# Two changes in one: an attention-and-experts kernel gets a new start, a new split of its shared half steps and a new final layernorm

## The chip, the core and the metric

The kernel runs on one core of one Trainium2 chip, in float32 throughout. The metric is the device time of one execution in microseconds, as the median of several runs. The engines are TensorE (PE in the profile, its weight loads PEld), VectorE (DVE), ScalarE (ACT), GpSimd (POOL) and SyncE (SP), which here only issues DMAs.

## The reference

The input is 16 sequences of 512 tokens of 128 numbers. Cut to what matters:

```python
# attention
q, k, v = silu(x @ Wq), silu(x @ Wk), x @ Wv            # 16 heads of 8
q, k = [concat(t * cos(theta * pos), t * sin(theta * pos)) for t in (q, k)]
out = ((q @ k.T) * causal_mask) @ v                     # per head, no softmax
out = (out @ Wo) * sigmoid(x @ G1 @ G2)
x = layernorm(x + layernorm(out) * gamma + beta)        # eps 1e-5
# mixture of experts
xn = x * rsqrt(mean(x * x) + eps)
probs = softmax(xn @ router_w.T)
top2, weights = top_k(probs, 2)                         # weights normed to sum 1
routed = for each of 8 experts, its first 1280 tokens:  (silu(xg @ rg) * (xg @ ru)) @ rd, times weight
shared = (silu(x @ sg) * (x @ su)) @ sd                 # hidden width 1024
x = layernorm(x + shared + routed)
```

## The kernel before

The tokens are cut into NT = 64 tiles of P = 128, NC = 4 to a sequence, B = 16 sequences of N = 512. Nearly all of the program's order is written by hand: inside a `manual_schedule` each engine takes its instructions in the order in which the Python code emits them.

**Constants (from L214).** SP and ACT issue the first loads. theta's row is spread over the partitions by a matmul `pth` (L280); `angles(c, th)` (L299) makes, for the tile position c, the angle theta·pos reduced to ±π with nine VectorE operations, and `sines(c)` takes cosine and sine on ScalarE into `cst_tok`. ScalarE folds G1·G2 into the projection weights `W` (L288). Four padded buffers `vpad` are zeroed, two on POOL (L274) and two on ScalarE (L277). `beginning(t)` puts the sines of tiles 1, 2, 3 ahead of `project` in the first iterations.

**Attention loop, t = -2 .. 64.** An iteration handles several tiles at different depths: `project(t + 2)` (the matmul `pq`, L418, then on ScalarE Silu into `qk`, Tanh for the gate, copies into `vpad`; on VectorE the rotation into `hat`), `turn_over(t + 1)` (transposes `pt`, L458, and ScalarE's copies kT, q2, qT), `energies(t)` (`pe`, then VectorE's causal mask into `et`), `values(t - 1)` and `remember(t + 1)` (matmuls `pst`, L479, which go into the running state through VectorE and a POOL addition, L490). Every fourth iteration starts a generator `after(b)` for a finished sequence: Wo, gate, first layernorm, residual, second layernorm, transposition into x1T, router logits. It is advanced some steps per iteration. In it, POOL takes reciprocal roots as a power of -0.5 (`rstd_of`, L113) and one more such power for the router's root mean square (`rms`, L594). `route(b0, b1)` is another generator, for the sequences 0-5, 6-11 and 12-15: softmax, top 2, ranks by matmuls `pin` (L690) that wait for VectorE's `both` (L679), slot numbers. When it has ended, `scatter_behind` issues on POOL, two an iteration, indirect DMAs that write the tokens' rows into `xg_dram` by slot.

**Shared expert.** Its work is cut into 384 half steps in the list `feed`: for each sequence eight pairs of `gate_half` (matmul pg, L137, then ScalarE's Silu `sl`, L139) and `up_half` (matmul pu, L150, then VectorE's product `h`, L151), and eight `down_half` (four matmuls into pd, L160; two make a tile, which VectorE adds into x1T, L165). The downs of a sequence stand behind the first two pairs of the next. `shared(t)`, twice an iteration, takes a half step if the sequence at the head of `feed` is ready:

```python
ready[b] = t + (6 if b else 10)
```

After the loop a while loop goes on with one half step per pass until the last sequences are normed, routed and scattered. There a pass count `waited` decides when a routing generator that has said "wait" goes on to its matmuls.

**Experts.** `load_expert(0)` fetches weights and the scattered rows `xg`; `clear_rows` (VectorE) blanks the unused rows in three parts, `turn_rows` (L904, L905) transposes them into xgT. Then 8 experts of three parts each; rows go back through an indirect DMA into `y_dram`.

**Finish.** The half steps that are left are done one per pass. From ten half steps after the last return of rows, every second pass adds one of 32 sums (`add_up`, L961, two per sequence) and every pass takes one or two steps of the final layernorm (`an_end`), in lots of tiles: `finish_lot` (one step per tile of statistics, one for the reciprocal root, then nb, L985, and one step per tile of ScalarE's output `res`, L988, the last with the output's DMA). When the last gate has been issued, ScalarE's Sqrt takes the place of POOL's power (`rstd_by_root`, L119, L121).

```python
                an_end()
                if begun % 2 == 1 or not feed:
                    an_end()
```

PSUM has three banks for g, three for u and two for d (pd, ept, ped) in the experts and the finish.

Of the kernel before, what the change touches and what calls it, by code (L numbers as in the profile page):

```python
# [19 lines left out]
P = 128  # L20
# [27 lines left out]
def tile_kernel(  # L48
# [44 lines left out]
    rms = keep.tile([P, NT], F32, name="rms")  # L93
# [101 lines left out]
    with ExitStack() as ph:  # L195
# [21 lines left out]
        with tc.manual_schedule(engines=ORDERED):  # L217
            th_row = cst.tile([1, D + HALF], F32, name="th_row")
            nc.sync.dma_start(th_row, theta.unsqueeze(0))
# [15 lines left out]
            nc.vector.memset(half_pi, math.pi / 2)  # L235
            warm = cst.tile([P, 1], F32, name="warm")
# [36 lines left out]
            for vp in vpads[:2]:  # L273
                nc.gpsimd.memset(vp, 0.0)  # L274

# [3 lines left out]
            pth = ps_w.tile([P, D + HALF], F32, tag="w", name="pth")  # L279
            nc.tensor.matmul(pth, ones[0:1, :], th_row, start=True, stop=True)  # L280
            th_sb = wk1.tile([P, D + HALF], F32, tag="w", name="th_sb")
            nc.scalar.copy(th_sb, pth)
# [3 lines left out]
            for vp in vpads[2:]:  # L286
                nought(vp.rearrange("p a b d -> p (a b d)"), 640)
# [3 lines left out]

            cst_tok = cst.tile([P, NC, 2, 16, 2, 8], F32, name="cst_tok")
            scratch = hp.tile([P, 10, D + HALF], F32, tag="h", name="scratch")
            turns_of = wk1.tile([P, D + HALF], F32, tag="o", name="turns_of")
            nc.vector.tensor_scalar(turns_of, pth, 1.0 / (2.0 * math.pi), None, ALU.mult)

        def angles(c, th):  # L299

            a, size, k, whole = scratch[:, c], scratch[:, NC + c], scratch[:, 8], scratch[:, 9]
            both = ((slice(0, D), pos[:, 0, c : c + 1]), (slice(D, D + HALF), pos[:, 1, c : c + 1]))
            for m, at in both:
                nc.vector.tensor_scalar(k[:, m], turns_of[:, m], at, MAGIC, ALU.mult, ALU.add)
            nc.vector.tensor_scalar(whole, k, MAGIC, -C1, ALU.subtract, ALU.mult)
            for m, at in both:
                nc.vector.scalar_tensor_tensor(a[:, m], th[:, m], at, whole[:, m], ALU.mult, ALU.add)
            nc.vector.tensor_scalar(k, k, MAGIC, -C2, ALU.subtract, ALU.mult)
            nc.vector.tensor_tensor(a, a, k, ALU.add)
            nc.vector.scalar_tensor_tensor(size, a, -1.0, a, ALU.mult, ALU.max)  # L310
            nc.vector.tensor_scalar(a, a, -PI_BELOW, PI_BELOW, ALU.max, ALU.min)
# [4 lines left out]
        def sines(c):  # L316

            for s, (from_, scale, bias) in enumerate([(scratch[:, NC + c], -1.0, half_pi), (scratch[:, c], 1.0, 0.0)]):
# [13 lines left out]

        with tc.manual_schedule(engines=ORDERED):
            angles(0, pth)
            sines(0)
            angles(1, th_sb)
            same(0)

# [3 lines left out]
            nc.gpsimd.tensor_tensor(causal[:, 0:1], scratch[:, 0, 0:1], zcol, ALU.mult)  # L342
# [13 lines left out]
            for at in (0, HALF):  # L356
                rows = causal[at : at + HALF, :]
                nc.gpsimd.affine_select(
                    rows, rows, pattern=[[1, HALF]], compare_op=ALU.is_ge, fill=0.0, base=0, channel_multiplier=-1
                )  # L360
            expi = cst.tile([P, E], I32, name="expi")
# [27 lines left out]
        def beginning(t):  # L389

            if t == -1:
                sines(1)
            elif t == 0:
                angles(2, th_sb)
                sines(2)
            elif t == 1:
                angles(3, th_sb)
                sines(3)

# [15 lines left out]

# [697 lines left out]
```

## Time and profile before

| | |
|---|---|
| median of 17 runs | 854.47 us (852.81 to 857.84) |
| the profiled execution | 853.75 us |
| its span | 852.0 us |
| TensorE busy | 815.5 us, 96% of the span |
| VectorE busy | 538.0 us, 63% |
| ScalarE busy | 414.2 us, 49% |
| POOL busy | 361.2 us, 42% |
| mean granted TensorE clock | 0.991 |

The span runs from the first to the last instruction. Each engine's busy time is the sum over its instructions; a busy TensorE hides the others wherever they keep up with it. The page also cuts the span into 40 slices of 21.3 us with the busy tenths of each engine and the clock granted to TensorE. A line of the waits names who waits, in which line, for whom: the total, how many times, and the longest.

### The profile page before, as it was taken

Reading aid. Unit: us, or ns where it says so; the run is one execution under the profiler, and the core shown is the slowest. Engines: PE = TensorE matmul, PEld = TensorE weight load, DVE = VectorE, ACT = ScalarE, POOL = GpSimd, SP = SyncE. Lnnn points to the kernel's source line nnn. Section 1 sums busy time; section 2 is a strip of 40 time slices with the busy share of each in tenths; the row PEclk is TensorE's granted clock in tenths of the full one; section 3 lists DMA queues with packets and bytes.
Section 4 is the critical chain, followed back from the end, with each engine's and each line's share of the span. In section 5 each row is a group of like instructions: output and inputs, shape, how many; then the busy total and the mean of one; then the engine's idle time right before and its main releaser. Section 6 shows DMA issues by size and latency. Waiting matters only on the chain. (4 is left out here: it accounts for less than half of the span.)

```text
span 852.0 us, 25793 instructions
## 1 busy us (share of the span) xinstructions
PE 815.5 (96%) x10288; PEld 556.6 (65%) x10288; DVE 538.0 (63%) x1695; ACT 414.2 (49%) x1342; POOL 361.2 (42%) x512
## 2 busy tenths in 40 slices
PE   6899999989999999999999999999999999999996
PEld 4666667756766865755666666776777667765564
DVE  7688888889988788975433334443434443278864
ACT  5667776675676567534222221333333333323455
POOL 2233333322466767686766660433343333402110
PEclk9899999999999999999999999999999999999998
DMA  6011111110111110057000014212331110056512
GB/s 201 23 35 35 33 34 35 34 34 19 37 56 57 59 48 22 29 206 255 27 12 7 1 34 137 82 38 91 94 98 52 63 61 25 31 161 178 145 49 63
DMA packets 66395, 57.55 MB, mean 68 GB/s; under 512 B 6180, under 2 KB 55132, under 8 KB 66274
## 3 DMA queue, kind: packets, MB, share of 16 engines
q1 hardware_dynamic: 59474, 44.95, 17.4%
q0 software_dynamic: 6656, 10.69, 3.9%
q8 instruction: 81, 1.33, 0.7%
q14 instruction: 40, 0.33, 0.1%
q10 hardware_dynamic: 144, 0.26, 0.1%
HBM read 32.62 MB, written 26.48 MB: 69 GB/s over the span
## 5 line engine op out<-in xcount | busy, mean ns | idle before, releaser
L723 POOL DMA_INDIRECT xg_dram<-x,idx x128 | 128.8, 1006 | 40.2 <-issue 35.0
L934 POOL DMA_INDIRECT y_dram<-y,to x80 | 77.5, 969 | 158.1 <-ACT y L932 158.1
L151 DVE TENSOR_TENSOR h<-sl,pu 128x512 f32<-128x512 f32 x128 | 87.8, 686 | 84.5 <-PE pu L150 56.3
L139 ACT ACTIVATE sl<-pg 128x512 f32<-128x512 f32 x128 | 75.5, 594 | 118.1 <-PE pg L137 112.5
L150 PE MATMUL pu<-x1T,su_sb 128*128 128x512 f32 x256 | 130.9, 593 | 0.7 <-ACT sl L139 0.7
L137 PE MATMUL pg<-x1T,sg_sb 128*128 128x512 f32 x256 | 131.4, 595 | 0.0
L160 PE MATMUL pd<-sd_sb,h 128*128 128x128 f32 x1024 | 122.8, 276 | 4.4 <-DVE x1T L165 4.4
L1026 DVE TENSOR_TENSOR eh<-esl,peu 128x512 f32<-128x512 f32 (+1 forms) x96 | 57.5, 599 | 109.7 <-PE peu L1023 109.7
L160 PEld LDWEIGHTS pd<-sd_sb,h 128*128 128x128 f32 x1024 | 119.1, 192 | 11.3 <-issue 5.7
L113 POOL TENSOR_TENSOR rstd<-ve,neghalf 128x4 f32<-128x4 f32 x45 | 49.2, 1094 | 124.1 <-DVE ve L111 119.8
L928 PEld LDWEIGHTS ped<-rd,eh 128*128 128x128 f32 x640 | 84.0, 192 | 24.6 <-issue 22.5
L490 POOL TENSOR_TENSOR state<-state,add 128x128 f32<-128x128 f32 x96 | 44.1, 459 | 130.6 <-DVE add L488 128.0
L513 DVE TENSOR_TENSOR et<-pe,causal 128x256 f32<-128x256 f32 x256 | 90.4, 416 | 8.8 <-PE pe L505 8.5
L1021 PE MATMUL peg<-xgT,rg 128*128 128x512 f32 (+1 forms) x192 | 84.6, 522 | 0.0
L1023 PE MATMUL peu<-xgT,ru 128*128 128x512 f32 (+1 forms) x192 | 84.4, 521 | 0.0
L928 PE MATMUL ped<-rd,eh 128*128 128x128 f32 x640 | 84.3, 275 | 0.0
L1025 ACT ACTIVATE esl<-peg 128x512 f32<-128x512 f32 (+1 forms) x96 | 50.5, 526 | 55.0 <-PE peg L1021 52.3
L150 PEld LDWEIGHTS pu<-x1T,su_sb 128*128 128x128 f32 x256 | 45.7, 190 | 45.1 <-issue 39.0
L932 ACT ACTIVATE y<-ped,wt 128x128 f32<-128x128 f32 x80 | 29.4, 368 | 84.6 <-PE ped L928 84.6
L137 PEld LDWEIGHTS pg<-x1T,sg_sb 128*128 128x128 f32 x256 | 44.4, 191 | 36.9 <-issue 34.8
L418 PE MATMUL pq<-W,xT 128*128 128x384 f32 x128 | 61.4, 563 | 5.1 <-ACT qT L467 2.2
L445 DVE TENSOR_TENSOR hat<-qk,cst_tok 128x512 f32<-128x512 f32 x64 | 45.0, 702 | 25.6 <-ACT qk L427 25.5
(176 smaller groups left out, 1259.7 us busy)
## 6 DMA issues: line engine op xcount, KB each, us to landing
y_dram<-vpad SPq DMA_DIRECT2D x16, 512.0 KB, 7.1
y<-y_dram SPq DMA_DIRECT2D x32, 256.0 KB, 3.4
xT<-xt SPq DMA_DIRECT2D x15, 384.0 KB, 3.2
xg<-xg_dram SPq DMA_DIRECT2D x8, 660.0 KB, 4.3
x<-x SPq DMA_DIRECT2D x16, 256.0 KB, 3.4
o<-res SPq DMA_DIRECT2D x15, 256.0 KB, 2.3
xg_dram<-x,idx POOLq DMA_INDIRECT x128, 2.3
rg<-rg SPq DMA_DIRECT2D x8, 256.0 KB, 4.8
```

Of the source, the lines that this page charges most:

```text
L137: nc.tensor.matmul(pg, sg_sb[:, ts(i, P)], seq, start=True, stop=True)
L139: nc.scalar.activation(sl, pg, AF.Silu)
L150: nc.tensor.matmul(pu, su_sb[:, ts(i, P)], seq, start=True, stop=True)
L151: nc.vector.tensor_tensor(h[i // half][:, i % half, :], h.pop(("s", i)), pu, ALU.mult)
L160: nc.tensor.matmul(pd, h[k][:, i - k * half, ts(c, P)], sd_sb[:, i, :], start=(i == 0), stop=(i == IS // P - 1))
L418: nc.tensor.matmul(pq[:, :, 0:24], xts[b][:, c, 0:P], W[:, 0:384].rearrange("p (h n) -> p h n", n=24), start=True, stop=True)
L513: nc.vector.tensor_tensor(et.rearrange("p s i n -> p (s i) n"), pes[a, half].rearrange("p s i n -> p (s i) n"), causal.unsqueeze(1).to_bro ...
L723: i = nc.gpsimd.indirect_dma_start(out=xg_dram[:, :], out_offset=bass.IndirectOffsetOnAxis(ap=idx[:, k, t : t + 1], axis=0), in_=x1[:, t, ...
L928: nc.tensor.matmul(pd, h[:, i, ts(c, P)], got[e][2][:, i, :], start=(i == 0), stop=(i == IR // P - 1))
L934: i = nc.gpsimd.indirect_dma_start(out=y_dram[:, :], out_offset=bass.IndirectOffsetOnAxis(ap=to[:, at : at + 1], axis=0), in_=y, in_offset ...
L1021: nc.tensor.matmul(pg[:, :n], rg_sb[:, ts(i, P)], xgTs[e][:, ds(o0, n)], start=True, stop=True)
L1023: nc.tensor.matmul(pu[:, :n], ru_sb[:, ts(i, P)], xgTs[e][:, ds(o0, n)], start=True, stop=True)
```

## The change

It joins several edits. At the start, theta's row is loaded by ACT's queue; a second matmul gives theta/2π; the product theta·pos comes from ScalarE (`linear`), `angles` keeps six VectorE operations and the absolute value for the cosine goes to ScalarE; two `vpad` are zeroed by VectorE and POOL. `project` is split into `products`, `squash`, `gate`, `spread` and `turn`, and the first three iterations are written out in another order. All of the first phase lies in one `manual_schedule`. In `after(b)` the second layernorm's reciprocal root and rms come from one POOL power of 128x2x4, behind three more VectorE operations; the rms's own power and the operations before it go. The scatters stand ahead of `remember`. Sequence 0 is ready for its shared half steps four iterations earlier. `waited` goes to more than 3 rather than 1. Ahead of the experts six half steps are taken instead of four, with the clears between. With the earlier shared steps and the while loop's passes the same in number, the half steps taken before the experts' own part go from 270 to 280, and those left for after the experts from 114 to 104. In the finish `an_end` is called twice every pass, and the last four tiles make lots of 2, 1 and 1.

```diff
-            nc.sync.dma_start(th_row, theta.unsqueeze(0))
+            nc.scalar.dma_start(th_row, theta.unsqueeze(0))
...
+            by_turn = cst.tile([1, P], F32, name="by_turn")
+            nc.vector.memset(by_turn, 1.0 / (2.0 * math.pi))
...
+            nc.vector.memset(vpads[3], 0.0)
...
+            pth = ps_w.tile([P, 2, M], F32, tag="w", name="pth")
+            nc.tensor.matmul(pth[:, 0], ones[0:1, :], th_row, start=True, stop=True)
+            nc.tensor.matmul(pth[:, 1], by_turn, th_row, start=True, stop=True)
...
-            for vp in vpads[2:]:
-                nought(vp.rearrange("p a b d -> p (a b d)"), 640)
...
+            def linear(c):
+                for m, order in both:
+                    nc.scalar.activation(
+                        scratch[:, NC + c, m], pth[:, 0, m], AF.Copy, scale=pos[:, order, c : c + 1]
+                    )
+
+            linear(0)
+            linear(1)
+            nc.scalar.copy(turns_of, pth[:, 1])
...
-        def angles(c, th):
-
-            a, size, k, whole = scratch[:, c], scratch[:, NC + c], scratch[:, 8], scratch[:, 9]
-            both = ((slice(0, D), pos[:, 0, c : c + 1]), (slice(D, D + HALF), pos[:, 1, c : c + 1]))
-            for m, at in both:
-                nc.vector.tensor_scalar(k[:, m], turns_of[:, m], at, MAGIC, ALU.mult, ALU.add)
-            nc.vector.tensor_scalar(whole, k, MAGIC, -C1, ALU.subtract, ALU.mult)
-            for m, at in both:
-                nc.vector.scalar_tensor_tensor(a[:, m], th[:, m], at, whole[:, m], ALU.mult, ALU.add)
-            nc.vector.tensor_scalar(k, k, MAGIC, -C2, ALU.subtract, ALU.mult)
-            nc.vector.tensor_tensor(a, a, k, ALU.add)
-            nc.vector.scalar_tensor_tensor(size, a, -1.0, a, ALU.mult, ALU.max)
-            nc.vector.tensor_scalar(a, a, -PI_BELOW, PI_BELOW, ALU.max, ALU.min)
+            for c in range(2, NC):
+                linear(c)
+
+        def angles(c, turns):
+
+            a, k = scratch[:, c], scratch[:, 8 + c % 2]
+            for m, order in both:
+                nc.vector.tensor_scalar(a[:, m], turns[:, m], pos[:, order, c : c + 1], MAGIC, ALU.mult, ALU.add)
+            nc.vector.tensor_scalar(k, a, MAGIC, None, ALU.subtract)
+            nc.vector.scalar_tensor_tensor(a, k, -C1, scratch[:, NC + c], ALU.mult, ALU.add)
+            nc.vector.scalar_tensor_tensor(a, k, -C2, a, ALU.mult, ALU.add)
+            nc.vector.tensor_scalar(k, a, -PI_BELOW, PI_BELOW, ALU.max, ALU.min)
...
+            nc.scalar.activation(scratch[:, NC + c], scratch[:, c], AF.Abs)
...
+            nc.gpsimd.memset(vpads[2], 0.0)
...
        def project(t):
+            products(t)
+            squash(t)
+            gate(t)
+            spread(t)
+            if t == NC - 1:
+                sines(t)
+            turn(t)
...
-            r2 = rstd_of(mv2[:, :, 1], NC, LN_EPS)
+
+            ve = small.tile([P, 2, NC], F32, tag="ve2", name="ve2")
+            nc.vector.tensor_scalar(ve[:, 0], mv2[:, :, 1], LN_EPS, None, ALU.add)
+            inv = small.tile([P, NC], F32, tag="sq", name="inv")
+            nc.vector.reciprocal(inv, ve[:, 0])
+            nc.vector.tensor_tensor(inv, inv, mv2[:, :, 1], ALU.mult)
+            nc.vector.tensor_scalar(ve[:, 1], inv, RMS_EPS, None, ALU.add)
+            nc.gpsimd.tensor_tensor(
+                norms[:, :, mine], ve, neghalf[:, : 2 * NC].rearrange("p (k c) -> p k c", k=2), ALU.pow
+            )
+            r2 = norms[:, 0, mine]
...
-            sq = small.tile([P, NC], F32, tag="sq", name="sq")
-            nc.vector.tensor_tensor(sq, r2, r2, ALU.mult)
-            nc.vector.tensor_tensor(sq, sq, mv2[:, :, 1], ALU.mult)
-            nc.vector.tensor_scalar(sq, sq, RMS_EPS, None, ALU.add)
-            nc.gpsimd.tensor_tensor(rms[:, mine], sq, neghalf[:, :NC], ALU.pow)
...
+            products(0)
+            products(1)
+            sines(0)
+            squash(0)
+            turn(0)
+            spread(0)
+            gate(0)
+            sines(1)
+            turn_over(0)
+            angles(2, turns_of)
+            remember(0)
+            squash(1)
+            turn(1)
+            spread(1)
+            gate(1)
+            energies(0)
+            products(2)
+            turn_over(1)
+            remember(1)
+            angles(3, turns_of)
+            sines(2)
+            squash(2)
+            turn(2)
+            spread(2)
+            gate(2)
+            nc.vector.tensor_scalar(wo_sb, wo_sb, 0.5, None, ALU.mult)
+            for t in range(1, NT + 1):
...
+                if left:
+
+                    scatter_behind(oTs[(t - 1) // NC][:, ds((t - 1) % NC * P, 1)])
+                    scatter_behind()
                 if 0 <= t + 1 < NT:
                     remember(t + 1)
-                if left:
-
-                    scatter_behind(oTs[(t - 1) // NC][:, ds((t - 1) % NC * P, 1)])
-                    scatter_behind()
...
-                    ready[b] = t + (6 if b else 10)
+                    ready[b] = t + 6
...
-                if waited > 1:
+                if waited > 3:
...
-        lots = [(b * NC, b * NC + NC) for b in range(B - 1)] + [(t, t + 1) for t in range(NT - NC, NT)]
+        lots = [(b * NC, b * NC + NC) for b in range(B - 1)] + [(NT - 4, NT - 2), (NT - 2, NT - 1), (NT - 1, NT)]
...
-            for o0, n in parts:
-                clear_rows(0, o0, n)
-            for _ in range(4):
-                feed.pop(0)[2]()
+
+            for n_before, cleared in ((4, parts[:2]), (2, parts[2:])):
+                for _ in range(n_before):
+                    feed.pop(0)[2]()
+                for o0, n in cleared:
+                    clear_rows(0, o0, n)
...
-                if begun % 2 == 1 or not feed:
-                    an_end()
+                an_end()
```

## The prediction

> **What bounds the kernel.** I read the page's busy table and slices first, then TensorE's idle stretches one by one, then busy time by stage, then the waits of those stages and the end of the timeline.
>
> ```profile
> span 852.0 us, 25793 instructions
> ...
> PE 815.5 (96%) x10288; PEld 556.6 (65%) x10288; DVE 538.0 (63%) x1695; ACT 414.2 (49%) x1342; POOL 361.2 (42%) x512
> ...
> PE   6899999989999999999999999999999999999996
> ...
> PEclk9899999999999999999999999999999999999998
> ```
>
> TensorE (PE) is busy for 815.5 of 852.0 us, so 36.5 us is all that re-ordering can win, plus what runs at a low clock. The thin slices are the first two and the last. The change removes no TensorE work.
>
> The stages (columns: stretch, length, then each engine's busy time, PEclk, DMA share, GB/s):
>
> ```profile
> 17.60:21.00 3.40, 3.40 (x48) 2.36 (x50) 3.31 (x12) 0.97 (x3) 1.02 (x2) 0.50 0.27 81
> 21.00:24.40 3.40, 1.34 (x72) 0.92 (x67) 2.39 (x7) 2.56 (x14) 0.00 (x0) 1.00 0.10 39
> 24.40:31.30 6.90, 5.98 (x105) 4.38 (x105) 3.34 (x10) 3.85 (x17) 0.91 (x2) 0.51 0.01 2
> 61.45:79.85 18.40, 16.44 (x479) 12.12 (x478) 15.74 (x60) 13.16 (x58) 7.42 (x11) 1.00 0.13 39
> 79.85:101.85 22.00, 22.00 (x495) 13.97 (x493) 17.87 (x63) 15.56 (x62) 6.92 (x10) 1.00 0.11 33
> 753.10:804.70 51.60, 48.54 (x248) 32.72 (x248) 43.99 (x142) 19.70 (x44) 8.66 (x8) 1.00 0.57 163
> ```
>
> At the start 10.3 us run at half clock. Four iterations without shared half steps (t=10..13) take 18.40 us, four with eight of them (t=14..17) 22.00 us at a full TensorE. In the finish VectorE (DVE) is busy for 43.99 of 51.60 us, so it has 7.6 us to spare there and TensorE 3.1.
>
> What TensorE waits for at the start, then around the experts' start, then in the finish (total us, times, longest):
>
> ```profile
> PE pst L479 <- ACT vpad L441: 2.0, 1, 2.0
> PE pt L458 <- DVE cst_tok L331: 1.6, 1, 1.6
> PE pq L418 <- ACT vpad L441: 1.5, 1, 1.5
> PE pq L418 <- ACT qT L467: 0.9, 1, 0.9
> ```
> ```profile
> PE pd L160 <- DVE x1T L165: 1.4, 1, 1.4
> PE pin L690 <- DVE both L679: 1.3, 1, 1.3
> PE ept L904 <- DVE xgT L905: 0.6, 1, 0.6
> ```
> ```profile
> DVE h L151 <- ACT sl L139: 5.5, 6, 1.0
> ...
> PE pd L160 <- DVE x1T L165: 3.1, 2, 1.6
> ```
>
> And the end, where after the last TensorE work one lot of one tile follows another:
>
> ```profile
> 843.25 0.28 PE L160 MATMUL pd<-sd_sb,h 128*128 128x128 f32 x1
> 843.56 0.29 DVE L165 TENSOR_TENSOR x1T<-pd,x 128x128 f32<-128x128 f32 x1 [0.34 <-PE pd L160]
> 843.77 0.28 DVE L105 BATCH_NORM_STATS2 st<-x1T 128x6 f32<-128x128 f32 x1
> ...
> 847.70 0.29 DVE L105 BATCH_NORM_STATS2 st<-x1T 128x6 f32<-128x128 f32 x1
> ```
>
> The execution with this profile took 853.75 us, 1.7 outside its span, and 0.7 less than the median of 854.47. I sum against 853.75 and add the 0.7 at the end. A measurement can tell about 0.2% (1.7 us) from no change.
>
> **1. The start.** VectorE's angles shrink from 9 operations a tile to 6 and the sines of tile 0 go ahead of its Silu. The chain to the first turn: six VectorE operations of 0.25 to 0.45 (1.7 us) after pth at 3.5, Abs and four sines (1.3), which end at 6.6; Silu of tile 0 waits for its projection until 7.1 and takes 0.55; same and hat take 0.9; with the handovers pt(0) stands at 8.85, and was at 10.41 with the 1.56 us wait above. ScalarE (ACT) loses two zeroings of 0.73, which go to VectorE and POOL in idle time, and gains per tile two linear copies and an Abs of about 0.3. Gone with re-ordering are at most the four waits above, 1.6+2.0+1.5+0.9 = 6.0 us up to the projection of tile 5 at 31.29. The new chains of ACT behind pt(2) (kT, Abs and sines, Silu, hat) and ahead of the projection of tile 4 (qT of tile 2) give about 0.9 back: −5.2, tile 5 at about 26. Ends: −3 if the half clock falls on more of the work, −7 if it falls on less. Abs has no row; by the nearest (0.3 for a copy) it costs 0.3 a tile.
> The trace shows 3.4 us slices at 0.50, each after a slice with TensorE less than three quarters busy. [...]
> [...] No row here shows Abs.
>
> **2. Shared half steps from t=10.** t=10..13 go from 18.40 to 22.00: +3.6. The eight half steps leave the stage after the experts, where they cost 0.858 (gate, up) to 0.914 (down) each: −7.0. Together −3.4. It needs VectorE to keep up in t=10..13 (17.9 of 22.0 busy in the four that already do this). Ends −3.6 and −2.5.
>
> **3. The third group's routing.** Its pin matmuls come four half steps (3.4 us) later than now and waited 1.29: −1.3. Nothing is queued behind them that would end later, since the scatters behind it are paced by the loop, whose 164 half steps stay. Ends −1.3 and 0.
>
> **4. The experts' first rows.** Now VectorE stands at the clears until xg lands, which holds back x1T (1.36) and xgT (0.57), 1.93 in all. With six half steps, four of them ahead of the clears, xg has landed some 4 us before. But clear 0 and 1 (0.6 each) and the next h (0.6), clear 2 (0.34) and xgT's copy (0.6) are a VectorE chain behind TensorE's last up half step; about 1.3 of it lies bare: −0.6. Ends −1.9 and +0.5.
>
> **5. The finish.** Two end steps every half step instead of three in two. While the 32 adds last (62 half steps) that moves 32 end steps forward, so VectorE must do more in the same half steps, and only two pd banks stand between it and TensorE: a pd waits for the x1T of two tiles before. From the first add (half step 14 after the experts) to the pd of half step 57: TensorE needs 30 × 0.858 + 12 × 0.914 = 36.7. VectorE, by spacing in the trace: 20 adds × 0.60 + 15 h × 0.60 + 5 x1T × 0.20 + 32 statistics × 0.40 + 8 ve × 0.13 + 7 nb × 0.15 = 36.9, the h it begins with 0.7, and idle time for sl behind res (the 5.5 us above, about 1.0 each): four lots here have res directly ahead of a sl, 4.0. That is 41.6, so TensorE waits 4.9. From there to half step 81: VectorE 12 × 0.60 + 8 × 0.60 + 4 × 0.20 + 20 × 0.40 + 5 × 0.13 + 4 × 0.15 = 22.05 and 3 × 1.0, TensorE 16 × 0.858 + 8 × 0.914 = 21.0: it waits 4.0. In all 8.9 where now it waits 3.1: +5.9. Ends: 0 if the idle time for sl vanishes, +8 at 1.5 us for each.
>
> **6. The end.** With the backlog done earlier and lots of 2, 1, 1, only the last tile's lot follows the last pd. Its statistics start at 843.77 instead of 847.70; the rest of the chain is the same: −3.9. Ends −3.9 and −2.7 (one lot more).
>
> **7. POOL.** The second norm's pow has eight columns where the nearest row has four (1.09); it replaces that pow and the one of rms (16 × 1.04). Bounds 1.04 and 2.1. Three small VectorE operations stand ahead of it (0.5), so r2 comes 0.5 to 1.5 later. By the trace TensorE's next need stands 0.8 us off in the few iterations without shared half steps and 3.5 us off in the others; the while loop has one TensorE wait behind it already (0.7 at 371), which may grow. The scatters now precede the state adds (two of 0.46), 2.4 us later on POOL; the next values needs them an iteration (4.6 to 5.5 us) on. +0.5, ends −0.5 and +2.
>
> Sum: −5.2 −3.4 −1.3 −0.6 +5.9 −3.9 +0.5 = −8.0: 845.75 against 853.75, 846.5 against the median.
>
> **Rivals.** *The finish absorbs it:* ScalarE's res no longer lands ahead of sl, TensorE waits 3 us as now: 846.5 − 5.9 = 840.6. For it: VectorE has 7.6 us to spare per 51.6. Against it: its work alone passes TensorE's in the sum of 5. *The start wins little:* half clock covers the time won, or the chain of ACT is the bound: term 1 at −1, 850.7. For it: ScalarE gets 12 operations more in the first 20 us; against: VectorE gave them up and ACT is busy for 3.85 of 6.9 us there. *Slower:* in the finish each lot's four res stand in one piece ahead of a sl, and VectorE idles for 4 × 0.41 + 0.59 = 2.2 us per lot. Over 12 lots while adds last that is 26 us of idle time where I counted 7: TensorE waits 28 instead of 9, +19, 865. It decides against the change from 8 us more than I counted, that is at 1.25 us of idle time per lot over all 12 lots. For it: the 5.5 us of such waits now. Against: res comes in pairs, a half step apart, with sl between. *It doesn't do what it says:* the clears are still reached before xg lands and the pin still waits: terms 3 and 4 at 0, 848.4; this lies in the forecast's range.
>
> **Chances.** The forecast 0.62 (843 to 850 alone), the finish that absorbs 0.15, the start that wins little 0.14, slower 0.06, others 0.03. The range from 841 to 852 takes in the first three and the ends of the terms (−3 to −7 and 0 to +8 carry most of it). Faster by over 0.2%: 0.89; within: 0.05; slower: 0.06.
>
> **What would show it.** Right: tile 5's projection at 26; t=10..13 taking 22 us; no wait of pin; statistics of the last tile right behind its x1T, so that the span ends some 4.6 us after the last pd, not 8.5; waits of pd for x1T of 9 us in three places of the finish; POOL some 16 us less busy. Wrong: waits of pd of 3 us (then the first rival) or over 17 (then slower); Abs with table loads; tile 5 after 29.

## The result, and the profile after

The changed kernel takes 861.0 us (median of 7 runs, 858.9 to 863.1) where the kernel before takes 854.54 (40 runs): a ratio of 1.0075, with a 95% interval of 1.0063 to 1.0088. It is 6.5 us slower; 846.5 was forecast, with 841 to 852 as the range. The profiled execution took 861.99 us with a span of 860.2.

The page of the changed kernel:

```profile
span 860.2 us, 25760 instructions
...
PE 819.7 (95%) x10290; PEld 557.9 (65%) x10290; DVE 536.8 (62%) x1680; ACT 415.1 (48%) x1349; POOL 360.8 (42%) x499
```

That line is not the whole truth, since busy time also grows when the clock falls: the same 32 matmuls of pe take 0.69 us in one execution of the kernel before (at 190.5 us, at a clock of 1.00) and 1.16 in another (before_again, at 188.7, at 0.53). The stages (stretch, length, busy time of PE, PEld, DVE, ACT, POOL, then PEclk, DMA share, GB/s) tell more:

```profile
0.00:29.91 29.91, 21.39 (x339) 15.09 (x339) 18.24 (x64) 20.16 (x89) 6.85 (x27) 0.89 0.47 145
60.66:83.35 22.69, 22.31 (x496) 14.05 (x494) 18.18 (x63) 15.53 (x62) 6.56 (x9) 1.00 0.11 32
801.61:806.01 4.40, 0.00 (x1) 0.01 (x1) 4.23 (x16) 1.21 (x4) 0.15 (x1) 0.99 0.53 159
805.96:809.37 3.41, 3.36 (x16) 3.37 (x16) 3.02 (x12) 1.48 (x4) 1.50 (x2) 0.50 0.82 238
828.74:832.57 3.83, 0.00 (x1) 0.00 (x0) 3.07 (x14) 0.85 (x2) 0.07 (x1) 1.00 0.23 68
833.27:836.68 3.41, 3.41 (x19) 3.41 (x18) 1.48 (x9) 1.01 (x3) 0.24 (x1) 0.50 0.26 77
```

The first line ends at the projection of tile 5 (31.29 us before); the second is t=10..13 (18.40 before, 22.0 forecast). The next four are the finish: TensorE stands for 4.40 us while VectorE is busy for 4.23 of them, and right behind it 3.41 us run at a clock of 0.50; then the same again with 3.83 us.

TensorE's waits over the whole span, and the end:

```profile
PE pd L161 <- DVE x1T L166: 9.6, 3, 4.4
...
PE po L580 <- ACT vpad L465: 2.6, 6, 0.5
PE pt L485 <- DVE wo_sb L846: 2.2, 1, 2.2
...
PE pt L485 <- DVE hat L472: 2.0, 1, 2.0
```
```profile
855.53 0.29 DVE L166 TENSOR_TENSOR x1T<-pd,x 128x128 f32<-128x128 f32 x1 [0.23 <-PE pd L161]
...
855.86 0.29 DVE L106 BATCH_NORM_STATS2 st<-x1T 128x6 f32<-128x128 f32 x1
...
857.17 0.49 ACT L1044 ACTIVATE res<-x1T,nb,rstd 128x128 f32<-128x128 f32 x1 [0.47 <-DVE nb L1041]
```

The last tile's statistics stand right behind its x1T, and pin waits no more. Both are as forecast.

Where the time went, by marks on TensorE in the two traces (stage length before and after):

| stage | before | after | change | forecast |
|---|---|---|---|---|
| up to the projection of tile 5 | 31.29 | 29.91 | -1.4 | -5.2 |
| tile 5 to 12 | 30.16 | 30.75 | +0.6 | 0 |
| tile 12 to 16 (t=10..13) | 18.40 | 22.69 | +4.3 | +3.6 |
| tile 16 to 63 (the last) | 269.33 | 273.55 | +4.2 | 0 to 0.5 |
| to the last router logits | 41.54 | 43.91 | +2.4 | 0 |
| to the experts' first matmul, two half steps more | 132.91 | 133.27 | +0.4 | -0.2 |
| experts | 219.34 | 219.33 | 0 | 0 |
| to the last pd, ten half steps fewer | 100.55 | 102.08 | +1.5 | -2.8 |
| to the end of the span | 8.52 | 4.76 | -3.8 | -3.9 |

The changes add up to +8.2, the forecast to -8.0. Three stages carry most of the miss: the start, the loop, the finish. A fourth was forecast at nothing and is not followed below, the 2.4 us up to the last router logits: ready_alone takes 42.9 us there and best 42.7, where best_late takes 41.2, so that about 1.4 of them come with the earlier half steps.

### The profile page after: what moved, and what is told of

It is laid out like the page before. It is cut to its first block, busy times and chain, and to the rows that moved or that the text cites. A ratio compares the mean times of both kernels' runs of the same rounds, so it can differ in the third digit from the quotient of the medians.

```text
span 860.2 us, 25760 instructions
## 1 busy us (share of the span) xinstructions
PE 819.7 (95%) x10290; PEld 557.9 (65%) x10290; DVE 536.8 (62%) x1680; ACT 415.1 (48%) x1349; POOL 360.8 (42%) x499
## 4 chain that ended last, share of the span: by engine, by line
PE 74%; DVE 17%; ACT 5%; issue 3%; POOL 1%; DVEq 0%; ACTq 0%; POOLq 0%
PE pd L161 11%; PE pu L151 10%; PE pg L138 10%; PE ped L984 8%; PE peg L1079 8%; PE peu L1081 8%; DVE et L540 4%; PE pq L432 4%; PE pe L532 3%; PE pt L485 2%; PE pout L565 2%; DVE st L106 2%; DVE h L152 2%; PE pst L506 2%; PE po L580 1%
## 5 line engine op out<-in xcount | busy, mean ns | idle before, releaser
L161 PE MATMUL pd<-sd_sb,h 128*128 128x128 f32 x1024 | 125.9, 280 | 9.6 <-DVE x1T L166 9.6
L161 PEld LDWEIGHTS pd<-sd_sb,h 128*128 128x128 f32 x1024 | 122.2, 196 | 15.9 <-DVE x1T L166 10.2
L517 POOL TENSOR_TENSOR state<-state,add 128x128 f32<-128x128 f32 x96 | 46.5, 484 | 108.6 <-DVE add L515 105.7
L114 POOL TENSOR_TENSOR rstd<-ve,neghalf 128x4 f32<-128x4 f32 x31 | 32.1, 1037 | 121.1 <-DVE ve L112 94.5
L472 DVE TENSOR_TENSOR hat<-qk,cst_tok 128x512 f32<-128x512 f32 x64 | 52.4, 818 | 36.2 <-ACT qk L444 35.8
```

The costliest lines, as they stand in the source:

```text
L161: nc.tensor.matmul(pd, h[k][:, i - k * half, ts(c, P)], sd_sb[:, i, :], start=(i == 0), stop=(i == IS // P - 1))
```

## The experiments

A ratio is against the kernel before, on the same chip, with its 95% interval. The kernel before took 854.7 to 855.1 us in three of the five groups of runs, and 864.4 (norms_apart, rate, bank, ready) and 866.6 (after_again, pow_late, start_alone, finish_alone) in the other two. The changed kernel loses much less on such a chip: its ratio there is 0.998 (after_again), not 1.0075. So a ratio from one of these eight runs is not set beside one from the other kind of chip; what carries over is read from the traces, iteration by iteration. Where an expectation speaks of "projection 62", it means the last one, of tile 63; "the loop" below runs from the projection of tile 12 to that of tile 63: 287.7 us before, 296.2 after.

**The norms.** Three kernels take the POOL power of eight columns apart. norms_apart puts the old code back:

```diff
-            ... ve, reciprocal, mult, add, power of 128x2x4
+            r2 = rstd_of(mv2[:, :, 1], NC, LN_EPS)
             normed_rows(0, 1)
+            ... sq = r2 * r2 * var + RMS_EPS, power of 128x4
```

> The changed kernel with the second layernorm's reciprocal root and rms taken apart again (POOL powers of four columns each, as before). Theory (each loss in the attention loop has its own cause, and the power of eight columns, 2.02 us against 1.04, holds back nb, ScalarE's normed rows and with them the next vpad and po): the waits of po for vpad (0.4 each) go, projection 62 comes about 4 us earlier than in the changed kernel (356.9), and the time falls from 861.0 to about 857. Rival (the shared half steps now meet other attention steps than before, since they begin four iterations earlier, and that alone makes the new waits): the power's length changes nothing that TensorE sees, 861 within 0.7.

Measured: 0.9917 (0.9899 to 0.9935), 858.07 us where the kernel before takes 864.36; the loop takes 289.2 us, 7.0 less than the changed kernel's. (bank and rate, which keep the wide power, have loops of 296.9 and 296.6 us on this same chip.) Of the six waits of po for vpad none is left. The loss of the loop went as the theory said, by more than the 4 us that it named. But the reason it gave (r2 late by the wide power) was still only argued. norms_split makes r2 early and leaves VectorE's operations where they are:

```diff
             nc.vector.tensor_scalar(ve[:, 0], mv2[:, :, 1], LN_EPS, None, ALU.add)
+            nc.gpsimd.tensor_tensor(norms[:, 0, mine], ve[:, 0], neghalf[:, :NC], ALU.pow)
             ... reciprocal, mult, add
-            ... power of 128x2x4
+            nc.gpsimd.tensor_tensor(norms[:, 1, mine], ve[:, 1], neghalf[:, :NC], ALU.pow)
```

> The changed kernel with the power of eight columns cut into two of four: the reciprocal root's right behind its own VectorE operation, the rms's behind the other three. Theory (what cost the loop its time is that r2 came a microsecond late, and nb, the normed rows, vpad and po behind it): the loop is as quick as in norms_apart (projection 62 about 347), time about that of norms_apart, 856 to 859. Rival (POOL's two microseconds in one place ahead of x + beta, or the three VectorE operations in that place, are what costs): the loop stays slow, projection 62 at 353 to 357, 861 to 863.

Measured: 1.006 (1.0043 to 1.0077), 859.54 us, loop 296.3 us: no better than the change. The theory of the late r2 fell. One iteration of norms_split, in the timeline of VectorE, POOL and TensorE:

```profile
95.79 0.17 DVE L605 TENSOR_SCALAR ve<-mv 128x4 f32<-128x4 f32 x1
95.99 0.18 DVE L608 RECIPROCAL inv<-ve 128x4 f32<-128x4 f32 x1
96.21 0.16 DVE L609 TENSOR_TENSOR inv<-inv,mv 128x4 f32<-128x4 f32 x1
96.40 0.17 DVE L610 TENSOR_SCALAR ve<-inv 128x4 f32<-128x4 f32 x1
96.48 0.68 DVE L472 TENSOR_TENSOR hat<-qk,cst_tok 128x512 f32<-128x512 f32 x1
...
99.40 0.16 DVE L616 SCALAR_TENSOR_TENSOR nb<-mv,norms 128x4 f32<-128x4 f32 x1
```
```profile
96.04 1.02 POOL L606 TENSOR_TENSOR norms<-ve,neghalf 128x4 f32<-128x4 f32 x1 [0.81 <-DVE ve L605]
```
```profile
101.59 1.16 PE L580 MATMUL po<-wo_sb,oT 128*128 128x128 f32 x8 [0.38 <-ACT vpad L465]
```

and the same place in norms_apart:

```profile
93.25 0.17 DVE L112 TENSOR_SCALAR ve<-mv 128x4 f32<-128x4 f32 x1
93.33 0.69 DVE L472 TENSOR_TENSOR hat<-qk,cst_tok 128x512 f32<-128x512 f32 x1
...
96.25 0.15 DVE L608 SCALAR_TENSOR_TENSOR nb<-mv,rstd 128x4 f32<-128x4 f32 x1
```

No DVE line from ve to nb has a bracket in these two stretches: VectorE is hardly idle there (0.1 us in all in norms_split). From ve to hat it is 0.69 us with the three operations and 0.08 without. r2 is ready at 97.1 in norms_split, and nb still comes only at 99.4, since et and the state's products are queued ahead of it. Behind nb stand ScalarE's normed rows, the next vpad and po, which waits 0.38. pow_late keeps the operations and moves only the second power back:

```diff
             normed_rows(0, 1)
+            nc.gpsimd.tensor_tensor(norms[:, 1, mine], ve[:, 1], neghalf[:, :NC], ALU.pow)
```

> As norms_split, but with the rms's power issued behind the first normed rows, where it stood in the kernel before; VectorE's three operations stay ahead. Theory (the three operations of 0.2 us stand in the one iteration in four in which VectorE has no idle time, and push et, the state's product and nb behind them): the loop stays slow, projection 62 at 354 to 357, time 857 to 860. Rival (without the rms's power ahead of it POOL's x + beta falls on the same time as hat, which then takes 1.3 us instead of 0.7): with the power back in its place hat takes 0.7 again and projection 62 comes at 347 to 349, time 851 to 854.

Measured: 0.9967 (0.9956 to 0.9977) on a chip on which the changed kernel itself has 0.9982 (after_again, below). hat is back at 0.72 us on average (0.82 in norms_split), and the loop still takes 298 us beside after_again's 297; from tile 13 to tile 59 no iteration of the two differs by more than 0.05 us. So it is neither the power's length nor its place, nor hat's longer time, but the VectorE operations. three_ops adds nothing but them to the kernel before:

```diff
             r2 = rstd_of(mv2[:, :, 1], NC, LN_EPS)
+            inv = small.tile([P, NC], F32, tag="inv", name="inv")
+            nc.vector.reciprocal(inv, mv2[:, :, 1])
+            nc.vector.tensor_tensor(inv, inv, mv2[:, :, 1], ALU.mult)
+            nc.vector.tensor_scalar(inv, inv, RMS_EPS, None, ALU.add)
```

> The kernel before with nothing but three more VectorE operations on 128x4 numbers behind the second layernorm's ve, where the change puts its own; their result is not used. Theory (VectorE has no idle time in that iteration, so that three times 0.2 us reach TensorE once a sequence): once in four iterations po waits for vpad by about 0.4 us, the loop from projection 12 to 62 grows by 5 to 9 us over 287.7, the time by 0.6 to 1.0%. Rival (what made the loop slow is something else in the change, the order or the width): no change within 0.2%.

Measured: 1.0032 (1.0018 to 1.0046), 857.45 beside 855.12 us; the loop takes 291.0 us, +3.3, and eight iterations (one of them just ahead of the loop) each grow by 0.47 to 0.49. In the kernel before VectorE is idle for at most 0.07 us between ve and nb in these eight; six other sequences did not grow by more than 0.1, and in five of them it is idle there for 0.15 to 0.38 us. The direction held, the size did not: it is half of what the same operations cost in the changed kernel. The half steps that begin four iterations earlier in the changed kernel do not make the other half, for it is there without them too: ready and best_late (below) both begin them late and differ in the loop in the norms alone, and their loops take 297.6 and 288.4 us (on different chips). Of these 9.2 us 2.7 lie in two iterations in which ready has a window of half clock, and 6.5 are left, as many as between norms_split and norms_scat with the early half steps. What makes it is open; in ready the same four iterations (11, 15, 19 and 23) grow by 0.59 to 0.60 where three_ops has 0.47 to 0.49.

**The finish.** rate undoes the two end steps a pass, finish_alone makes them (and the lots) the only change:

```diff
                 an_end()
-                an_end()
+                if begun % 2 == 1 or not feed:
+                    an_end()
```

> The changed kernel with three end steps in two half steps as before, lots of 2, 1, 1 kept. Theory (VectorE is overloaded by two end steps a half step; TensorE's stops of 4.4 and 3.8 us then bring two windows of 3.4 us at half clock): waits of pd for x1T fall from 9.6 to about 3, no half-clock window in the finish (-3.4), the end behind the last pd grows by 1 to 4: about 853.5 (852 to 856). Rival (the same VectorE work only waits somewhere else): pd's waits move to later half steps, 859 to 861.

Measured: 0.9975 (0.9965 to 0.9986), 862.19 us. The waits of pd fall to 3.6 us, no window of half clock is left in the finish up to the last pd, and the stage up to it takes 92.65 us instead of 102.08. But the end then follows 13.1 us behind, not 4.8: +8.3 eats nearly all of the 9.4. The first half of the theory held, the price of the backlog was mis-sized.

> The kernel before with only the finish changed: two end steps every half step and lots of 2, 1, 1. Theory (VectorE is overloaded while sums are added): waits of pd for x1T of 8 to 9.5 us instead of 3.1, the largest above 4 us and followed by half clock; the span ends 4.8 us behind the last pd instead of 8.5: +6 of waits, +1.7 to +3.4 of half clock, -3.8 at the end, about 859. Rival (the end steps had to be done anyway, the earlier the better): 851 to 854.

Measured: 1.006 (1.0038 to 1.0082), 872.14 beside 866.58 us. What follows its two stops of pd, of 3.3 and 4.3 us (columns as above):

```profile
793.28:800.11 6.83, 5.83 (x27) 5.83 (x28) 5.31 (x21) 3.29 (x8) 1.94 (x2) 0.50 0.56 167
...
820.59:827.42 6.83, 4.89 (x23) 4.89 (x24) 6.05 (x24) 1.65 (x4) 2.56 (x2) 0.50 0.66 193
```

The edit alone loses 5.6 us: waits of 7.6, and two stretches at a clock of 0.50 that are twice as long as those of the changed kernel.

**The start.**

```diff
-            nc.tensor.matmul(pth[:, 1], by_turn, th_row, start=True, stop=True)
+            pturn = ps_e.tile(...)   # a PSUM bank of its own
+            nc.tensor.matmul(pturn, by_turn, th_row, start=True, stop=True)
...
-            angles(0, pth[:, 1])
+            angles(0, pturn)
```

> The changed kernel with theta over 2 pi in a PSUM bank of its own, so that VectorE's first angles do not share a bank with ScalarE's eight linear copies. Theory (the angles of tile 0 stood behind all eight copies because both engines read pth, until 6.2 us): angles(0) begin at about 3.8, pt(0) comes at about 9.3 instead of 11.0, the time falls by about 1.5 to 859.5. Rival (the chain through ScalarE and the projection of tile 0 sets pt(0) anyway): pt(0) stays at 10.5 or later, 861 within 0.5.

The changed kernel's first angles and first turn, then those of bank:

```profile
6.20 0.54 DVE L320 TENSOR_SCALAR scratch<-pth,pos 128x128 f32<-128x128 f32 x2 [2.83 <-ACT scratch L302]
11.02 1.09 PE L485 MATMUL pt<-ident,hat 128*128 128x128 f32 x4 [1.96 <-DVE hat L472]
```
```profile
4.55 0.54 DVE L321 TENSOR_SCALAR scratch<-pturn,pos 128x128 f32<-128x128 f32 x2 [0.22 <-ACT turns_of L309]
9.38 0.63 PE L486 MATMUL pt<-ident,hat 128*128 128x128 f32 x4 [1.26 <-DVE hat L473]
```

In the changed kernel VectorE waits 2.83 us for ScalarE's copies, although its first operation reads nothing that they write (its third reads what the first two of the eight write); with a bank of its own it starts at 4.55 (it still shares that bank with the one copy of turns_of), and the first turn comes 1.6 us earlier. Measured: 0.9985 (0.9976 to 0.9993), 863.01 us. That this wait goes with a bank of its own is shown (2.83 us against 0.22); the time can't be told from that of the changed kernel (0.9982 in after_again, on another chip of the slower kind). In this trace tile 5 comes 3.9 us earlier than in the changed kernel's. The finish, whose two half-clock stretches are 6.8 us long instead of 3.4, takes 1.6 us more up to the last pd, and the loop and the two stages behind it take 0.7 and 1.8 more; that last part is not explained.

> Of the whole change only the start: everything else as in the kernel before. Theory (the start wins 1 to 2.5 us, since VectorE's first angles stand behind ScalarE's eight copies from the same PSUM tile): projection 5 at 28 to 30, time about 853 where the kernel before has 854.5. Rival (the start's gain is lost again in the loop, as all TensorE waits only come earlier): 854.5 within 0.7.

Measured: 0.9976 (0.9965 to 0.9987), 2.1 us. Tile 5 at 27.6, and from there to tile 26 no iteration differs from the kernel before by more than 0.02 us: a gain at the start is kept. It is a quarter of what the best kernel gains in all.

**The earlier half steps.** ready takes them out of the change, ready_alone puts only them into the kernel before (the one line of ready[b]).

> The changed kernel with sequence 0 ready four iterations later, as before: eight half steps go back behind the experts. Theory (eight half steps cost 4.3 us in t=10..13 and 7.0 behind the experts, the waits of the loop are due to the wide power): t=10..13 take 18.4 us again, the rest of the loop keeps its added waits, 861.0 + 2.7 = 863.7. Rival (the shift by four iterations makes the new waits of the loop): about 3.5 us of waits go as well, 860.

Measured: 1.0049 (1.0036 to 1.0062), 868.95 us. t=10..13 take 19.0 us, and the stage behind the experts 109.4 instead of 102.1, as the theory's prices had it. But from tile 16 to 63 it loses 5 us more than the changed kernel, and the time was 868.95 where 863.7 was expected. Two waits of po of 1.9 us stand there that the kernel before has too, but here a window of 3.41 us at a clock of 0.50 follows each: these two iterations take 2.7 us more than in best_late, which has the same two waits and no such window.

> The kernel before with sequence 0 ready four iterations earlier and nothing else. Theory (eight half steps cost 3.6 us in iterations 10 to 13 and 7.0 behind the experts): iterations 10 to 13 take 22.0 us, and the time falls by 3.4 us, 0.4%. Rival (with eight half steps less TensorE waits more for VectorE in the finish, and the end shows it): within 1 us of the kernel before.

Measured: 1.0066 (1.0046 to 1.0085), 860.4 us, slower where 3.4 us faster was expected. t=10..13 take 22.06 as forecast, and the later iterations win 1.2 back. TensorE's waits ahead of the experts:

```profile
PE pu L150 <- DVE h L151: 3.5, 1, 3.5
PE pg L137 <- DVE h L151: 0.8, 1, 0.8
```

VectorE stands at the clears until xg lands, as before, but the half steps beside it are now gate and up, which need VectorE's h at once; pd had two banks of slack. Two windows (6.8 us) of half clock follow. And the end comes 11.8 us behind the last pd instead of 8.5, because with fewer passes fewer end steps are taken on the way. ready_clears adds the change's new place of the clears:

```diff
-                    ready[b] = t + (6 if b else 10)
+                    ready[b] = t + 6
...
-            for o0, n in parts:
-                clear_rows(0, o0, n)
-            for _ in range(4):
-                feed.pop(0)[2]()
+            for n_before, cleared in ((4, parts[:2]), (2, parts[2:])):
+                ...
```

> The kernel before with two parts of the change together: sequence 0 ready four iterations earlier, and six half steps with the clears between them ahead of the experts' first rows. Theory (ready_alone lost its gain where the clears wait for xg with only gate and up half steps beside them, 3.5 and 0.9 us and two windows of half clock; the clears' new place takes that away): no wait above 1 us there, no half clock, 5 to 7 us less than ready_alone, 0.995 to 1.001 of the kernel before; the end behind the last pd grows further, to about 13 us, and eats most of the half steps' gain. Rival (the loss of ready_alone lies elsewhere): 1.005 or more.

Measured: 1.0017 (1.0007 to 1.0027), 855.84 us: the wait is gone (0.9 twice), no half clock there, and the end stands 13.5 us behind the last pd. The mechanism held; the time came out just above the range (0.995 to 1.001), 4.6 us below ready_alone where 5 to 7 were expected. t=10..13 take 23.5 us here instead of 22.1, with a window of half clock at 60.6 us.

**A version that beats both.** best has the norms apart, theta over 2 pi in its own bank, and an end step less in every third pass:

```diff
                 an_end()
-                an_end()
+                if begun % 3 or not adds or not feed:
+                    an_end()
```

> The changed kernel with the norms apart, theta over 2 pi in its own bank, and, while sums are left to add, two end steps in two of three passes and one in the third. Theory (each loss has its own cause, and the causes add): pd waits for x1T three times by less than 2 us each, 5.5 in all, so that no window of half clock follows; the span ends about 6 us behind the last pd; 858.1 of norms_apart less 1.5 at the start, less 3.4 of the finish, less up to 3.4 of half clock: about 850 (848 to 853). Rival (VectorE's work in the finish is what ends last, whatever its order): 855 to 858.

Measured: 0.9895 (0.9878 to 0.9911), 845.75 beside 854.69 us, better than expected. pd waits 5.4 us in three places, the largest 2.2; one window of half clock remains, behind that one. The end is 5.9 us behind the last pd.

> The version of best once more, beside best_scat and on another chip if it falls so: 0.989 of the kernel before on a chip on which that takes 854.5, and no more than that ratio on one on which it takes 864 to 867.

0.9887 (0.9868 to 0.9907) on another chip. One of the kind on which the kernel before takes 864 was not met again, so that this half of the expectation stays untested.

> The version of best with the scatters behind the state additions again, as in the kernel before. Theory (the scatters' place moves POOL's state by 2.4 us, and pout has more slack than that): within 1 us of best beside it. Rival (it matters in the last iterations and in those with scatters): 2 us less than best.

0.9874 (0.9845 to 0.9902), where best_again has 0.9887 on the same chip: the place of the scatters makes no difference that the intervals show.

> The changed kernel with the two norms apart and with the scatters behind the state additions again. Theory (scatters ahead of the state additions hold POOL's state back, and pout waits for it in the last iterations, 2.0 us between 362 and 369 us of norms_apart): these waits go, 2 us less than norms_apart, about 856. Rival (they are waits for VectorE's et, which the products h of the half steps now stand ahead of): nothing changes, within 1 us of norms_apart.

0.9982 (0.997 to 0.9994). It ran on another chip than norms_apart, and the waits of pout that it was to remove were absent from best too, which keeps the scatters ahead. So they came with something else than the order. Beside norms_split, on the same chip, the run shows the price of the norms once more: 853.87 us against 859.54, with loops of 289.8 and 296.3 (best_scat, next to last, shows no effect of the scatters' place).

> The version of best with sequence 0 ready four iterations later, as in the kernel before. Theory (with the finish relieved, eight half steps moved out of it are worth 3.5 us there; they cost 3.7 us in iterations 10 to 13, and spare 1.6 us of waits later in the loop): 1 to 3 us more than best, 847 to 849 where the kernel before takes 855. Rival (the finish is bound by VectorE, and the move is worth nothing): 845.5 or less.

0.9904 (0.9887 to 0.9921), 845.73 us: with everything else mended the earlier half steps are worth nothing. The time is next to the rival's, but its reason (a finish in which the move wins nothing) is not what the traces show. Against best_again, on the same chip, the earlier half steps win 4.0 us in the stage behind the experts and 2.3 from tile 16 to 63, where two waits of po of 1.9 us return without them; they pay 3.7 in t=10..13 (22.1 instead of 18.4), 1.5 up to the last router logits and 1.2 behind the last pd.

**Bases.** after_again and before_again are the two kernels themselves.

> The changed kernel itself, beside the next three on the same chip, as their base. Expected at 861 within 1.5, with two or more windows of half clock behind the stops of pd at 4.4 and 3.8 us.

864.4 us, where the kernel before took 866.58: 0.9982 (0.9971 to 0.9992). On this chip the change is a hair faster.

> The kernel before itself, to see what its time on this chip is made of: it took 864 beside the last four kernels where it took 854.5 elsewhere. Theory (it waits in one place for rows that are scattered and fetched again through DRAM, and that takes longer here): the clears ahead of the experts' first rows begin later against the last scatter, and x1T and TensorE behind them. Rival (windows of half clock): more of them in its record.

854.4 us, on a chip where it takes 854.7. It fell on the other kind of chip than the one it was meant to look at, so that neither theory was tested. It shows something else: in the profile of before the two waits of po of 1.9 us are followed by no half clock, in this one each is followed by 3.41 us at 0.50, and these two iterations take 1.26 and 1.20 us longer.

## Why the prediction was wrong

**1, the start: -5.2 forecast, -1.4 found.** The step that failed is "six VectorE operations ... after pth at 3.5". They began at 6.20, behind all eight of ScalarE's copies from the same PSUM tile; the first turn came at 11.0, not 8.85, and later than before (10.4). bank shows the wait. Up to tile 5, 10.2 us run at half clock in the profile of before and 6.8 in that of after. How far half clock moves the term (its ends of −3 and −7) was my estimate; no run shows that share by itself, only the spread of the whole: in nine profiles with this same start tile 5 comes between 27.6 and 30.0 us (28.6 on average), in six with the old start between 29.5 and 31.9 (30.7), so that the start wins about 2.1 us, which is also what start_alone shows, and the -1.4 is that of one pair of profiles. In the five profiles with theta over 2 pi in its own bank tile 5 comes between 26.0 and 27.2 (26.8): most of what the term lacks is this one wait. A stop of 2.2 us ahead of tile 2's turn, whose hat stands behind the angles of tile 3 on VectorE, was not in the sum either, which gives back 0.9 for other chains. The sum counts no table load for Abs, which has no row in the profile before; in both profiles ScalarE has eight, of 1.28 us each, none of them at Abs, which takes 0.37 us a tile where 0.3 was counted.

**2, the earlier half steps: -3.4.** The 3.6 us in t=10..13 were right to 0.1 once the norms are apart (22.05). The other half was wrong: half steps moved away from the finish take passes away from it, in which the end steps are done, and so come back as backlog (13.5 us behind the last pd in ready_clears) or as VectorE's overload. Which half steps then stand beside the clears was not followed at all, and ready_alone paid 4.3 us and two half-clock windows for it. The part of the change with the clears is what repairs that. In best against best_late the move wins 4.0 us behind the experts, not 7.0, and gives 1.2 of them back behind the last pd.

**3, pin: -1.3,** right; no such wait is left. **4, the first rows: -0.6.** 0.88 twice is 1.76 where 1.3 was forecast: the chain is there, its price 0.4 too low.

**5, the finish: +5.9 forecast.** The sum of waits was right: 8.9 forecast, 9.6 found, at three pd. What failed is that it stopped at the waits. Each of the two long ones is followed by 3.41 us at a clock of 0.50 with TensorE busy for 3.36 and 3.41 us of it; by an estimate from length and clock that costs half of it, 1.7 us each, 3.4 in all. The same slices were in front of me at the start of the trace of before, and I used them only there. All half-clock stretches that begin ahead of the last pd in these traces are 3.413 us long, or two or four times that, and the same stops came with one such window or with two: the stop of 4.40 us with 3.41 us in the changed kernel, that of 4.34 with 6.83 in finish_alone.

**6, the end: -3.9,** found -3.8.

**7, the power: +0.5 forecast, about 7 found in the loop.** The prediction named the three VectorE operations and their 0.5 us and then followed them only into r2. It did not look at what is queued behind them on VectorE, which in that iteration has no idle time: hat, h, et, the state's products and nb. The bounds of the term came from slack between POOL and TensorE, and that was the wrong engine: with r2 early (norms_split) nothing is won. Half of the 7 is what three_ops shows for these operations alone; what makes the other half is open. The table shows less than 7 because other iterations got shorter: from tile 16 to 63 norms_apart takes 267.2 us, the kernel before 269.3. POOL, for which 16 us less was named as a sign, is as busy as before (360.8 us, 361.2 before), since the power of eight columns takes 1.90 us on average where those of four take 1.04 to 1.09.

The rival on the slower side was a larger wait in the finish, decided from 8 us more than counted. The finish up to the last pd did turn out 4.3 us worse than its sum, the norms 6.5, the start 3.8 (3.1 by the averages): the change was lost by three terms, not by the one mechanism that the rival had.

## What to carry to other kernels

Cost an added operation on every engine by the stretch of its queue in which it stands: three operations of 0.2 us cost next to nothing in some sequences and 0.16 to 0.2 us each in others, mostly according to whether that engine is idle there, and the average share (63% here) does not tell. A stop of TensorE can cost more than itself, since the clock can fall behind it. In the 20 profiles, behind the first 35 us, all 19 stops of 3.3 us or more were followed by one or two windows of 3.41 us at 0.50, and so were 7 of the 15 stops of 1.9 to 2.2 us; of the 60 stops of 1.0 to 1.87 us none was. One and the same stop of 1.9 us cost 1.2 us more in one execution than in another. Three more windows, between 56 and 61 us in best_scat, pow_late and ready_clears, came with no stop of 1 us ahead of them, so that long stops are not the only way there. And work that covers something else (half steps that carry end steps along) is not won by moving it away: count what it covered.

## What was not expected of the hardware

A POOL power of 128x8 numbers takes 1.90 us on average in the profile of after, where those of 128x4 take 1.04 (rms) and 1.09 (rstd) in that of before.

Windows of half clock move the time of one and the same kernel: before and before_again show it at the two waits of po (1.26 and 1.20 us more where 3.41 us at 0.50 follow each). The six executions of norms_apart, of which only one was traced, have spans of 851.9 and 852.3 us at a mean clock of 0.994, and of 856.3 to 856.8 at 0.986. That windows make this difference too is likely, not shown.

The kernel before takes 854.5 to 855.1 us on some chips and 864.4 or 866.6 on others. On the latter TensorE stops at pout without a releaser that the profile shows, for 1.3 to 2.2 us in all in norms_apart, rate, bank, ready and after_again, for 6.2 in start_alone, and in finish_alone:

```profile
PE pout L538 <- issue: 6.1, 16, 0.5
```

No such line stands among the waits of the kernel before's profile here. The changed kernel loses only 3.4 us on such a chip (864.4 against 861.0), so that there it is not slower. What TensorE waits for in these places is open.
